# Where the causal mask is added in a fused two-layer attention kernel, and scores cut at the diagonal

## The chip, the cores and the metric

The kernel runs on one core of a Trainium2 chip. The metric is the device time in microseconds of one execution; a time given for a kernel is the median of its runs. A profile is one execution taken by the hardware profiler; it lists every instruction of the engines TensorE (PE; its weight loads are listed apart as PEld), VectorE (DVE), ScalarE (ACT), GpSimd (POOL) and SyncE (SP) with start and end.

## The reference, cut to what matters

There are two layers over x of shape 8 x 512 x 256. Each is x + attention(norm(x)) + ffn(norm(x)). Attention has 16 heads of 16 features over 512 tokens; the change touches that of layer 1, which is causal and is done twice on the same keys and values, the second time with queries that come out of a convolution over the first result:

```python
def _causal_attn(q, k, v):
    scale = 1.0 / math.sqrt(q.shape[-1])
    scores = jnp.einsum('bthd,bshd->bhts', q, k) * scale
    t = q.shape[1]
    mask = jnp.tril(jnp.ones((t, t), dtype=bool))
    scores = jnp.where(mask, scores, -jnp.inf)
    attn = jax.nn.softmax(scores, axis=-1)
    return jnp.einsum('bhts,bshd->bthd', attn, v)
...
ctx = _causal_attn(q, k, v)
conv_out = conv(ctx, conv_w, taps=3) + conv_b
ctx2 = _causal_attn(conv_out, k, v)
out = ctx2 @ out_w.T + out_b
```

Layer 0 has attention without a mask and a feed-forward part with eight routed experts; layer 1 a low-rank feed-forward part with gelu. Everything is in fp32.

## The kernel before, in words

Attention is cut into jobs (`Job`, L372) of one batch and four heads. Each head has 16 features, kept on 32 partitions, so that the four heads of a job lie on the four groups of 32 rows of TensorE, and the scores of up to four heads can run beside each other. Layer 0 has 32 jobs of 8 steps, layer 1 has 64 jobs of 6 steps (32 for the first attention, 32 for the second). All steps of both layers form one joined run of numbered steps (`run`, L490).

A job passes twice over its scores. In the first pass, `scores` (L384), queries lie on the partitions of the result; VectorE takes each row's maximum (L414, in layer 1 with a causal mask added from SBUF, L416). `shift` (L423) then transposes the maxima on TensorE (L426), VectorE copies them (L429), and four small DMAs on SP's queue (L433) write them into a spare row of the queries. In the second pass, `exps` (L435), twelve steps (`LEAD`) after the first, keys lie on the partitions, the shift is part of the product, and ScalarE takes the exponential out of the bank (L469). `attend` (L475) multiplies the exponentials with the values (L482).

In layer 1 a step of either pass works on two heads (one pair of row groups, `pr`), and the two passes of a step are on opposite pairs, so that four row groups are busy at once. What blocks a step takes is in `MX_SEQ` and `SC_SEQ` (L81 to L89): a block of keys `kc` needs only the queries from `lo = 128 kc` on, so key block 0 is 512 columns wide, block 1 is 384 and shares a bank with block 3 of 128, and block 2 is 256. The steps of a job take block 0, then blocks 3 and 1, then block 2, first for one pair of heads and then for the other. The first pass has the same widths in the same order.

The causal mask of the second pass concerns only the first 128 columns of each block, which lie on the diagonal. `mask_t` (L206) is two copies of a 128 x 128 triangle of 0 and -1e30 in bf16. In `exps`, after the scores of both heads, two matmuls (L463) with the bf16 identity as weights add `mask_t` to the bank: 128 columns per head for a step with one block, 256 for one with two. The exponentials wait for them. In a bank with two blocks, the one at column 128 is multiplied first, so that the mask's columns of both blocks are at the front.

The order of the work is the program's own (no scheduler moves instructions on an engine). A step is: scores of the first and the second pass, block by block in turn (L525, `zip` over both lists); then what follows each (maxima on VectorE; masks and exponentials); then filling work out of `todo` (L536); then the attends that are due. `fill_evenly` (L151) spreads the filling work (projections L347, values L356, convolution L1124, gelu part L1047 and L1075, transposes L320, L426 and L1142, output projection L1174) by due time and cost over the steps that are `free` (L508): four of each six. The other two have attends (key block 0 in one; 1, 3 and 2 in the next). So nearly every step has either filling work or attends behind its masks.

The PSUM banks are dealt out by rings (`share_banks`): in the joined run three banks for the first pass, three for the second (`sc`), one for the attends, one or two for the rest (L261, L265). At `t == end`, when the first passes are over, `banks_last` (L269) gives the second pass five.

In the twelve steps in which layer 1 has begun and the second pass still belongs to layer 0, the first pass has steps of two blocks and the second only of one. `zip` stops at the shorter list, so there the second block of the first pass, query chunk 0 of the first two jobs, isn't multiplied: 8 matmuls. The maxima of those rows are then those of what the bank held, which only changes by what the softmax is shifted.

Of the kernel before, what the change touches and what calls it, by code (L numbers as in the profile page):

```python
# [1 line left out]

# [17 lines left out]
P = 128  # L20
NB = 8
S = 512
# [5 lines left out]
PH = 32  # L28
# [52 lines left out]
SC_SEQ = (  # L81
    [((i // 2,), 1 - i % 2) for i in range(8)],
    [((0,), 0), ((3, 1), 0), ((2,), 0), ((0,), 1), ((3, 1), 1), ((2,), 1)],
    [((0,), 0), ((0,), 1), ((3, 1), 0), ((3, 1), 1), ((2,), 0), ((2,), 1)],
)
# [94 lines left out]
def block_kernel(ctx: ExitStack, tc: tile.TileContext, x, a0_wqk, a0_bqk, a0_wv, a0_bv, cent, experts,  # L180
                 a1_wqk, a1_bqk, a1_wv, a1_bv, conv_w, conv_b, out_w, out_b, u1, v1, f_b1, u2, v2, f_b2, out):
    nc = tc.nc
# [20 lines left out]
    ident_bf = const.tile([P, P], BF16, name="ident_bf")  # L203
    nc.vector.tensor_copy(ident_bf, ident)

    mask_t = const.tile([P, 2 * P], BF16, name="mask_t")  # L206
# [26 lines left out]
    def take_turn(kind):  # L233
        turn[kind].append(turn[kind].pop(0))
        return turn[kind][-1]
# [13 lines left out]
    def share_banks(**kinds):  # L249

        rings.update({k: list(v) for k, v in kinds.items()})

    def bank(kind="mm"):
        rings[kind].append(rings[kind].pop(0))
        return rings[kind][-1]
# [5 lines left out]
    def banks_alone():  # L261
        share_banks(mx=banks[:3], sc=banks[3:6], av=banks[6:7], mm=banks[7:])


    def banks_between(free):  # L265
        share_banks(mm=banks[6:] if free else banks[7:])


    def banks_last():  # L269
        share_banks(sc=banks[:5], av=banks[6:7], mm=banks[5:6] + banks[7:])  # L270
# [4 lines left out]
    class Norms:  # L275
# [4 lines left out]
        def __init__(self, pool, bs, nm, twice):  # L280
            self.bs, self.nm, self.twice = bs, nm, twice
            n = len(bs) * NC
            self.mv = pool.tile([P, n, 2], F32, name=f"mv{nm}", bufs=1)
            self.rs = pool.tile([P, 2 if twice else 1, n], F32, name=f"rs{nm}", bufs=1)
            self.rs1 = pool.tile([P, n], F32, name=f"rs1{nm}", bufs=1) if twice else None
            self.nm2 = pool.tile([P, n], F32, name=f"nn{nm}", bufs=1) if twice else None
            self.nm_t = pool.tile([P, n], F32, name=f"nm{nm}", bufs=1)
# [84 lines left out]
    class Job:  # L372


        def __init__(self, nm, causal, scale, v, g, done):
            self.nm, self.causal, self.scale, self.v, self.g, self.done = nm, causal, scale, v, g, done
            self.q = self.k = None
            self.m = None
            self.seq = int(causal)
            self.shift_row = (HD, 0)[g % 2]  # L380
            self.e = {}
            self.av = None

        def scores(self, i):  # L384
# [38 lines left out]
        def shift(self):  # L423
# [8 lines left out]
            for c in range(NC):  # L432
                nc.sync.dma_start(out=self.q[self.shift_row : P : PH, c * P : (c + 1) * P], in_=mT[4 * c : 4 * c + 4, :])  # L433

        def exps(self, i):  # L435
            blocks, pr = SC_SEQ[self.seq][i]
            heads = [bank("sc") for _ in range(2)]
            parts, at = [], 0
            for kc in blocks:
                lo = kc * P if self.causal else 0  # L440
                parts.append((kc, at, lo))
                at += S - lo
            mm = [
                [
                    lambda h=h, kc=kc, at=at, lo=lo: nc.tensor.matmul(  # L445
                        heads[h % 2][:, at : at + S - lo],
                        lhsT=self.k[h * PH : (h + 1) * PH, kc * P : (kc + 1) * P],
                        rhs=self.q[h * PH : (h + 1) * PH, lo:],
                        start=kc == blocks[-1],
                        stop=not self.causal,  # L450
                    )
                    for h in (2 * pr, 2 * pr + 1)
                ]
                for kc, at, lo in reversed(parts)
            ]
            n = at

            def after():
                if self.causal:


                    for h in range(2):
                        nc.tensor.matmul(  # L463
                            heads[h][:, : len(blocks) * P], lhsT=ident_bf, rhs=mask_t[:, : len(blocks) * P],
                            start=False, stop=True,
                        )
                e = take_turn("e" if n == S else "e2")
                for h in range(2):
                    nc.scalar.activation(e[:, h, :], heads[h][:, :n], AF.Exp, scale=self.scale)  # L469
                for kc, at, lo in parts:  # L470
                    self.e[kc, pr] = e[:, :, at : at + S - lo]

            return mm, after
# [16 lines left out]
    def run(jobs0, jobs1, todo):  # L490
        end = T0 + STEPS[1] * len(jobs1)
        for job in jobs1[-(LEAD // STEPS[1]) :]:
            job.seq = 2
        mx_at, sc_at, attends = {}, {}, {}
        for layer, jobs in enumerate((jobs0, jobs1)):
            for j, job in enumerate(jobs):
                t0 = layer * T0 + STEPS[layer] * j
                for i in range(STEPS[layer]):

                    t = t0 + i  # L500
                    mx_at.setdefault(t if t >= LEAD else t - t % 2, []).append((job, i))
                    t += LEAD
                    sc_at.setdefault(t if t < end else t - (t - end) % 2, []).append((job, i))
                av_at = AV_AT[job.seq]
                for i, blocks in av_at.items():
                    attends.setdefault(LEAD + t0 + i, []).append((job, blocks, i == max(av_at)))

        def free(t):  # L508

            return t < TS or 0 < (t - TS) % STEPS[1] < 5  # L510

        todo.first()
        for t in range(max(attends) + 1):
            todo.t = t
            if t == LEAD:
                banks_alone()
            if t == end:
                banks_last()
            mm, after = [], []
            for at, call in ((mx_at, Job.scores), (sc_at, Job.exps)):  # L520
                for job, i in at.get(t, ()):
                    m, a = call(job, i)
                    mm.append(m)
                    after.append(a)
            for together in zip(*mm):  # L525
                for m in together:
                    for f in m:
                        f()
            for f in after:
                f()  # L530
            if t >= end:
                todo.fill(t, 99.0, 1)
            elif "pool" in l1:
                if t >= TS + STEPS[1]:
                    banks_between(free(t))
                todo.fill_evenly(t, free)  # L536
            else:
                todo.fill(t, MOE_PER_STEP, 99)
            for job, blocks, last in attends.get(t, ()):
                for kc in blocks:  # L540
                    job.attend(kc, kc == 0, last and kc == blocks[-1])
                if last:
                    job.done(job, t)
        todo.drain()

    norms_of = {}
# [55 lines left out]
    if True:  # L602
# [338 lines left out]
        for b in range(NB):  # L941
            for g in range(HG):
                job = Job(f"0_{b}_{g}", False, 1.0, vbuf[b % 2], g, l0_done)
# [287 lines left out]
    for n in range(NB * HG + LAG):  # L1231
        if n < NB * HG:
            l1_job(1, n)
        if n >= LAG:
            l1_job(2, n - LAG)
    l1["ready"] = features_ready
    run(jobs, jobs1, todo)


# [86 lines left out]
```

## Time and profile before

| what | value |
|---|---|
| median of 3 runs | 2138.09 us (2135.71 to 2151.41) |
| the profiled execution: its own time | 2149.31 us |
| its span, first to last instruction | 2147.5 us |
| TensorE busy | 1984.3 us, 92% |
| VectorE, ScalarE, GpSimd busy | 1252.2, 995.2, 403.1 us |
| granted TensorE clock, mean | 0.974 |
| masks of the second pass (L463) | 768 matmuls |

How to read a profile's row of a group: line, engine, operation, out<-in by the program's names, rows x columns of the array and the shape, count; then busy time in us and the mean length of one in ns; then the engine's idle time just before such instructions and who ended it. Matmuls are pipelined and their ends are modelled, so the lengths of neighbours overlap: two starts are compared rather than a start and an end. An fp32 matmul of the program stands in the trace as two matmuls (two passes), a bf16 one as one. In a row of the timeline, equal neighbours are merged (x4), and the columns are start in us from the span's start, length in us, and what. A row of waits says who waited for whom: us in total, times, and the longest.

Slices of the span (a digit is the busy share in tenths of one of 40 slices of 53.7 us) show that layer 1, from about 1000 us on, has TensorE busy at 9 tenths and VectorE at 6.

### The profile page before, as it was taken

Reading aid. Unit: us, or ns where it says so; the run is one execution under the profiler, and the core shown is the slowest. Engines: PE = TensorE matmul, PEld = TensorE weight load, DVE = VectorE, ACT = ScalarE, POOL = GpSimd, SP = SyncE. Lnnn points to the kernel's source line nnn. Section 1 sums busy time; section 2 is a strip of 40 time slices with the busy share of each in tenths; the row PEclk is TensorE's granted clock in tenths of the full one; section 3 lists DMA queues with packets and bytes.
Section 4 is the critical chain, followed back from the end, with each engine's and each line's share of the span. In section 5 each row is a group of like instructions: output and inputs, shape, how many; then the busy total and the mean of one; then the engine's idle time right before and its main releaser. Section 6 shows DMA issues by size and latency. Waiting matters only on the chain. (4 is left out here: it accounts for less than half of the span.)

```text
span 2147.5 us, 36982 instructions
## 1 busy us (share of the span) xinstructions
PE 1984.3 (92%) x14168; PEld 1027.1 (48%) x14168; DVE 1252.2 (58%) x3611; ACT 995.2 (46%) x1950; POOL 403.1 (19%) x414
## 2 busy tenths in 40 slices
PE   5797999999999999988999999899999999999998
PEld 3333555555555555543444544445445444454554
DVE  5564455555545554555666666666666665666663
ACT  4343333333333333335456564555565555545554
POOL 4153000000000000024355321222121222212100
PEclk8699999999999999997999999999999999999999
DMA  5013212132222122121000000000000000000000
GB/s 209 13 47 119 104 52 104 62 122 77 67 99 94 63 94 104 57 53 40 16 16 15 8 2 2 12 2 2 11 2 11 2 2 11 2 2 12 2 12 21
DMA packets 37201, 93.64 MB, mean 44 GB/s; under 512 B 5920, under 2 KB 28064, under 8 KB 34080
## 3 DMA queue, kind: packets, MB, share of 16 engines
q0 software_dynamic: 6384, 59.78, 7.6%
q1 hardware_dynamic: 29792, 30.56, 4.5%
q8 instruction: 111, 1.82, 0.4%
q10 hardware_dynamic: 848, 0.93, 0.1%
q14 instruction: 66, 0.54, 0.1%
HBM read 70.03 MB, written 20.45 MB: 42 GB/s over the span
## 5 line engine op out<-in xcount | busy, mean ns | idle before, releaser
L469 ACT ACTIVATE e<-bank 128x512 f32<-128x512 f32 (+1 forms) x1280 | 639.4, 552 | 830.6 <-PE bank L445 480.5
L397 PE MATMUL bank<-k,q 32*128 32x512 f32 (+1 forms) x3056 | 724.5, 536 | 25.5 <-DVE m L414 23.6
L416 DVE CUSTOM_DVE_ANT_0 junk<-bank,cmask 128x512 bf16<-128x512 f32 (+3 forms) x1024 | 502.5, 491 | 352.3 <-PE bank L397 277.2
L445 PE MATMUL bank<-q,k 32*128 32x512 f32 (+3 forms) x3072 | 685.9, 531 | 3.4 <-ACT e L469 3.1
L397 PEld LDWEIGHTS bank<-k,q 32*128 32x128 f32 x3056 | 267.7, 186 | 410.2 <-issue 160.1
L414 DVE TENSOR_REDUCE m<-bank 128x1 f32<-128x512 f32 x512 | 328.9, 685 | 159.2 <-PE bank L445 127.8
L482 PE MATMUL bank<-e,v 128*32 128x512 f32 (+3 forms) x3072 | 305.9, 500 | 8.9 <-ACT k L339 2.9
L445 PEld LDWEIGHTS bank<-q,k 32*128 32x128 f32 x3072 | 250.0, 185 | 16.5 <-ACT e L469 9.6
L1065 POOL TENSOR_SCALAR xT<-xT 128x512 f32<-128x512 f32 x64 | 95.3, 1489 | 605.5 <-ACT xT L1057 524.7
L829 PE MATMUL bank<-hsT,w 128*128 128x256 f32 x736 | 182.4, 394 | 6.9 <-DVE hsT L812 6.9
L829 PEld LDWEIGHTS bank<-hsT,w 128*128 128x128 f32 x736 | 135.5, 192 | 74.9 <-issue 59.1
L850 PE MATMUL bank<-w,hT 128*128 128x256 f32 x736 | 169.1, 383 | 0.0
L850 PEld LDWEIGHTS bank<-w,hT 128*128 128x128 f32 x736 | 136.1, 190 | 36.4 <-issue 19.7
L347 PE MATMUL bank<-xT,wqk 128*128 128x256 f32 (+1 forms) x384 | 134.2, 479 | 11.9 <-DVE q L337 4.8
L938 POOL TENSOR_TENSOR acc<-acc,og 128x256 f32<-128x256 f32 x32 | 23.2, 725 | 591.2 <-DVE og L934 591.1
L482 PEld LDWEIGHTS bank<-e,v 128*32 128x32 f32 x3072 | 71.5, 109 | 113.8 <-issue 89.4
L463 PE MATMUL bank<-mask_t,ident_bf 128*128 128x128 bf16 (+1 forms) x768 | 122.9, 243 | 0.0
L463 PEld LDWEIGHTS <-ident_bf 128*128 128x128 bf16 x768 | 43.9, 97 | 155.0 <-issue 139.7
L1124 PE MATMUL bank<-ctxT,cw 128*128 128x128 f32 x768 | 100.4, 281 | 13.1 <-DVE mT L429 11.2
L842 DVE TENSOR_SCALAR hT<-bank,w 128x256 f32<-128x256 f32 x92 | 44.5, 484 | 115.5 <-ACT hT L840 115.5
L1124 PEld LDWEIGHTS bank<-ctxT,cw 128*128 128x128 f32 x768 | 92.0, 194 | 23.3 <-DVE mT L429 14.3
L347 PEld LDWEIGHTS bank<-xT,wqk 128*128 128x128 f32 x384 | 68.8, 196 | 70.1 <-issue 42.2
(178 smaller groups left out, 1702.6 us busy)
## 6 DMA issues: line engine op xcount, KB each, us to landing
q<-mT SPq DMA_DIRECT2D x384, 2.0 KB
hs_d<-zeros SPq DMA_DIRECT2D x23, 256.0 KB
hs<-hs_d SPq DMA_DIRECT2D x23, 256.0 KB
fs_d<-f SPq DMA_DIRECT2D x23, 256.0 KB
acc<-in_x SPq DMA_DIRECT2D x8, 512.0 KB
out<-acc SPq DMA_DIRECT2D x8, 512.0 KB
cw<-in_conv_w SPq DMA_DIRECT2D x1, 768.0 KB
wqk<-in_a_wqk ACTq DMA_DIRECT2D x1, 512.0 KB
```

The source lines that it names most:

```text
L347: nc.tensor.matmul(ps, lhsT=w[:, k, col : col + P], rhs=src[:, k, tokens], start=(k == 0), stop=(k == 1))
L397: lambda h=h, qc=qc, at=at, nk=nk: nc.tensor.matmul(heads[h % 2][:, at : at + nk], lhsT=self.q[h * PH : (h + 1) * PH, qc * P : (qc + 1) * ...
L414: nc.vector.tensor_reduce(self.m[:, qc, h, :], src, AX.X, ALU.max, negate=True)
L416: nc.vector.tensor_tensor_reduce(out=l1["junk"][:, :nk], in0=src, in1=l1["cmask"][:, S - nk :], scale=1.0, scalar=-3e38, op0=ALU.add, op1= ...
L445: lambda h=h, kc=kc, at=at, lo=lo: nc.tensor.matmul(heads[h % 2][:, at : at + S - lo], lhsT=self.k[h * PH : (h + 1) * PH, kc * P : (kc + 1 ...
L463: nc.tensor.matmul(heads[h][:, : len(blocks) * P], lhsT=ident_bf, rhs=mask_t[:, : len(blocks) * P], start=False, stop=True,)
L469: nc.scalar.activation(e[:, h, :], heads[h][:, :n], AF.Exp, scale=self.scale)
L482: nc.tensor.matmul(self.av[h * PH : (h + 1) * PH, lo:], lhsT=self.v[:, kc, 4 * self.g + h, :], rhs=es[h // 2][:, h % 2, :], start=first, s ...
L829: nc.tensor.matmul(ps[:, i * TB : (i + 1) * TB], lhsT=w[:, O_W1 + k * FF + fc * P : O_W1 + k * FF + (fc + 1) * P], rhs=self.hsT[:, k, :], ...
L850: nc.tensor.matmul(ps[:, 0:D], lhsT=self.hT[:, fc, j * P : (j + 1) * P], rhs=w[:, O_W2 + fc * D : O_W2 + (fc + 1) * D], start=(fc == 0), s ...
L1065: nc.gpsimd.tensor_scalar(c, c, 1.0, None, ALU.add)
L1124: nc.tensor.matmul(ps, lhsT=l1["cw"][:, k, tap, c * P : (c + 1) * P], rhs=l1["ctxT"][b % 2][:, k, tap + lo : tap + lo + P], start=(k == 0 ...
```

## The change

The masks leave the end of `exps` for a function of their own, `masks`. It takes the two banks, and writes the mask into the first columns of both as the first matmuls of their group (`start=True`). `run` calls it at the end of a step, after filling work and attends, for the second pass of the next step. The scores then add to what the mask wrote. For this each block is cut at the diagonal: 128 columns that lie on the mask, and the rest, which are fresh columns. So a step's scores of 512 columns become pieces of 384 and 128; those of blocks 1 and 3 become 256, 128 and 128; those of block 2 become 128 and 128. The last piece to be issued is the diagonal one of the first block.

`zip` becomes `zip_longest`, since the lists of both passes now differ in length in every step; the eight left-out matmuls of the first pass are so put in. `banks_last` is called at the end of the step before `end`, ahead of the masks for `end`.

```diff
+        def masks(self, i):
+            n = len(SC_SEQ[self.seq][i][0]) * P
+            self.banks[i] = heads = [bank("sc") for _ in range(2)]
+            for h in heads:
+                nc.tensor.matmul(h[:, :n], lhsT=ident_bf, rhs=mask_t[:, :n], start=True, stop=False)
+
         def exps(self, i):
             blocks, pr = SC_SEQ[self.seq][i]
-            heads = [bank("sc") for _ in range(2)]
+            heads = self.banks.pop(i) if self.causal else [bank("sc") for _ in range(2)]
...
+            n = at
+            pieces = [(kc, at, lo, S) for kc, at, lo in parts]
+            if self.causal:
+                pieces = [(kc, at, lo, lo + P) for kc, at, lo in parts]
+                pieces += [(kc, at + P, lo + P, S) for kc, at, lo in parts if lo + P < S]
             mm = [
                 [
-                    lambda h=h, kc=kc, at=at, lo=lo: nc.tensor.matmul(
-                        heads[h % 2][:, at : at + S - lo],
+                    lambda h=h, kc=kc, at=at, lo=lo, hi=hi: nc.tensor.matmul(
+                        heads[h % 2][:, at : at + hi - lo],
                         lhsT=self.k[h * PH : (h + 1) * PH, kc * P : (kc + 1) * P],
-                        rhs=self.q[h * PH : (h + 1) * PH, lo:],
-                        start=kc == blocks[-1],
-                        stop=not self.causal,
+                        rhs=self.q[h * PH : (h + 1) * PH, lo:hi],
+                        start=not self.causal,
+                        stop=at == 0,
                     )
                     for h in (2 * pr, 2 * pr + 1)
                 ]
-                for kc, at, lo in reversed(parts)
+                for kc, at, lo, hi in reversed(pieces)
             ]
-            n = at
             def after():
-                if self.causal:
-                    for h in range(2):
-                        nc.tensor.matmul(
-                            heads[h][:, : len(blocks) * P], lhsT=ident_bf, rhs=mask_t[:, : len(blocks) * P],
-                            start=False, stop=True,
-                        )
                 e = take_turn("e" if n == S else "e2")
...
-            if t == end:
-                banks_last()
...
-            for together in zip(*mm):
+            for together in zip_longest(*mm, fillvalue=()):
...
                 if last:
                     job.done(job, t)
+            if t + 1 == end:
+                banks_last()
+            for job, i in sc_at.get(t + 1, ()):
+                if job.causal:
+                    job.masks(i)
```

More of the change, by code (lines that the diff above doesn't have):

```diff
@@ L1 @@
 from contextlib import ExitStack
+from itertools import zip_longest
 import concourse.bass as bass
@@ L381, in __init__ @@
             self.e = {}
+            self.banks = {}
             self.av = None
```

## The prediction

> **What bounds the kernel now.** I read the page's busy shares first, then the busy time by stretch, then the waits of layer 1, then TensorE's instructions in order of time.
>
> ```profile
> PE 1984.3 (92%) x14168; PEld 1027.1 (48%) x14168; DVE 1252.2 (58%) x3611; ACT 995.2 (46%) x1950; POOL 403.1 (19%) x414
> L463 PE MATMUL bank<-mask_t,ident_bf 128*128 128x128 bf16 (+1 forms) x768 | 122.9, 243 | 0.0
> ```
>
> ```profile
> 1500.00:1600.00 100.00, 94.43 (x834) 49.41 (x834) 66.04 (x236) 56.17 (x116) 18.86 (x13) 1.00 0.02 7
> ```
>
> Columns of the second: TensorE, its weight loads, VectorE, ScalarE, GpSimd, then granted clock and DMA. Layer 1 runs from about 1000 us to the end; its 384 steps of 2.75 us keep TensorE 94% busy at the full clock, so what an edit does to the order of TensorE's own work counts almost fully, unless TensorE waits there anyway. Its waits in layer 1:
>
> ```profile
> PE bank L1124 <- DVE mT L429: 11.2, 12, 1.7
> PE bank L426 <- ACT avs L1158: 7.0, 12, 1.9
> PE bank L445 <- ACT e L469: 2.6, 6, 1.2
> ACT e L469 <- PE bank L463: 335.4, 270, 4.5
> ```
>
> TensorE mostly waits for VectorE to empty the bank of the transposed maxima (L429). For the exponentials it hardly waits, although ScalarE waits 335 us for the mask: ScalarE has the slack. Then the steps themselves (start, length, what):
>
> ```profile
> 1506.63 0.28 PE L463 MATMUL bank<-mask_t,ident_bf 128*128 128x128 bf16 x2
> 1506.85 1.50 PE L482 MATMUL bank<-e,v 128*32 128x384 f32 x24
> 1508.28 0.59 PE L397 MATMUL bank<-k,q 32*128 32x384 f32 x2
> ...
> 1509.36 0.39 PE L463 MATMUL bank<-mask_t,ident_bf 128*128 128x256 bf16 x2
> ...
> 1515.03 0.70 PE L397 MATMUL bank<-k,q 32*128 32x512 f32 x2
> ...
> 1516.11 0.28 PE L463 MATMUL bank<-mask_t,ident_bf 128*128 128x128 bf16 x2
> ```
>
> The lengths overlap, so I use start to next start. Two things are to be seen. A group of scores of one 512-wide block per head takes 1516.11 - 1515.03 = 1.08 us, and one made of a 384 and a 128 block takes 1509.36 - 1508.28 = 1.08 us too. And the price of a mask depends on what stands behind it, as these show:
>
> ```profile
> 1018.31 1.13 PE L347 MATMUL bank<-xT,wqk 128*128 128x256 f32 x4
> 1019.37 0.59 PE L397 MATMUL bank<-k,q 32*128 32x384 f32 x2
> ...
> 1244.91 0.39 PE L463 MATMUL bank<-mask_t,ident_bf 128*128 128x256 bf16 x2
> 1245.14 1.03 PE L347 MATMUL bank<-xT,wqk 128*128 128x256 f32 x4
> 1246.10 0.48 PE L397 MATMUL bank<-k,q 32*128 32x256 f32 x2
> ...
> 1322.86 0.28 PE L463 MATMUL bank<-mask_t,ident_bf 128*128 128x128 bf16 x2
> 1322.98 1.04 PE L320 MATMUL bank<-ident,o 128*128 128x128 f32 x8
> ```
>
> The same projection, four passes of 256 columns, takes 1.06 us straight behind scores (1018.31) and 0.96 behind a mask (1245.14). The 0.10 is the load of its first weights, which lies bare after a change of tile shape, and which the mask covers today. So a narrow mask in front of a fill of full tile shape costs only 0.12 (1322.86 to 1322.98), of which 0.10 would be paid anyhow. In front of the attends (other tile shape, so TensorE empties first) it costs 0.22 (1506.63 to 1506.85).
>
> **The change part by part.** No other engine's instruction list changes; TensorE gets 776 more fp32 matmuls (768 pieces, 8 maxima), and its masks move.
>
> *Masks moved.* The prices: a 256-wide pair followed at once by scores took 0.322, a narrow pair followed by scores 0.215, in both about 0.10 of it the emptying of the array; so the columns alone are about 0.215 and 0.11. Counting the neighbours of each mask pair in TensorE's instruction order, before:
> - 123 narrow in front of attends x 0.215 = 26.4
> - 115 wide in front of fills x 0.229 = 26.3
> - 61 narrow in front of full-shape fills x 0.122 = 7.4
> - 61 narrow in front of gelu fills of another shape (L1047, L1075) x 0.215 = 13.1
> - 12 with no fill = 3.5; together 76.7 us.
>
> After (the mask stands behind the fill or the attends, in front of scores):
> - 157 narrow behind full-shape fills x 0.11 = 17.3; 38 wide x 0.215 = 8.2
> - 61 narrow behind attends x 0.215 = 13.1; 62 wide x 0.322 = 20.0
> - 23 wide behind L1047 x 0.322 = 7.4; 18 narrow behind narrow shapes x 0.215 = 3.9; 13 with no fill 2.9
> - and the bare first weights of 116 full-shape fills that now follow scores, x 0.10 = 11.6; the 63 transposes of maxima (L426) load 16 columns instead of 128, taken as 0.02 each = 1.3 (bounds 0 and 6.3).
>
> Together 85.7, so +9.0 us. The mask itself is not dearer; what it hid comes bare. The bounds are 0 (the load of the first weights goes partly behind the emptying) and +19 (0.05 more in each of 384 steps, should mask and scores not overlap as fill and scores do).
>
> *Cover lost in waiting steps.* In 64 steps the fill then waits for VectorE (45.9 us in all). Going through them, 11.9 us of the mask's time lay inside what would otherwise have been a longer wait. VectorE's queue is set by the scores, whose end does not move, so the fill waits that much longer and the mask comes on top behind it: +11.9, less 3 for bare weights that vanish in the same waits: +9 (bounds 0, if the next step's VectorE queue gives it back, and +12).
>
> *Split scores.* A piece more on the two row groups of the exponentials, while the maxima's row groups run their 512 or 384 + 128 columns. The trace has that very pair of pieces, at 1.08 against 1.08; to the nanosecond the medians are 7 to 9 ns apart: 384 x 0.008 = +3 us. A rule speaks against it: the Trainium skill, TensorEngine Tiling (Array Packing), section Performance Considerations (Instruction Overhead), gives each matmul some 60 cycles on trn2, 25 ns at the 2.4 GHz it states. With 388 pairs of pieces, two passes each, side by side in pairs, that would be an estimated +19 us, and the sum +37. I take the row, which is of this shape, and keep the rule for the range. What the trace lacks is two row groups going through three pieces while the two others do two.
>
> *Masks ahead of the bank.* The ring of scores has three banks in this stretch. The second mask of a step therefore waits for the first exponential of the step before. Behind it in TensorE's queue stand the maxima's scores, and behind these VectorE; before, only the exponentials' own scores waited, and the maxima ran meanwhile. In 53 of 368 steps the first exponential ends after the next scores begin. There a wait now costs mask and emptying behind it, about 0.2; but the exponentials begin earlier, since they no longer wait for the mask: they start 0.27 (narrow) or 0.32 us (wide) after the scores' group today, and 0.17 after it in layer 0, which has no mask (the median of 211 groups); so 0.10 to 0.15 earlier. In about half of the 53 ScalarE is behind with older work and nothing is gained; but the scores of all four row groups then run together, where a late pair ran on alone. Going through the 63 steps that come within reach of it, wins and losses leave +1; bounds -6 (0.1 in 60) and +12 (0.2 in 60). If ScalarE's slack were gone, each late exponential would delay the next step one for one.
>
> *Missing maxima.* Eight 128-wide matmuls in four steps, beside 512-wide scores of layer 0 on the other row groups: 1.07 us either way: 0.
>
> *The end.* In the last 35 us the chain of waits goes scores, mask, exponential, copy; the exponential comes 0.15 to 0.3 earlier some four times: -1.
>
> Sum: 9 + 9 + 3 + 1 - 1 = +21 us on the profiled execution's span of 2147.5 us (2149.3 with what lies around it), or 0.98%. The median of the runs, 2138.1, stands 0.5% below that execution, so I scale: 2138.1 x 1.0098 = 2159 us.
>
> **The rivals.**
> *The shorter chain wins (not slower).* Exponentials that start 0.12 earlier take away waits. For it: 24 us by which score groups are stretched where ScalarE is late, and 25 us of ScalarE waits in fills. Against it: in 315 of 368 steps the exponential is done in time. At 0.12 in each of 100 such places it is -12, which leaves 2147. If all 49 us went, because a wait breaks a longer queue behind it, 2138 + 21 - 49 = 2110; it is faster than before once more than 21 us of the 49 go.
> *Splitting is dear.* If the loads of the extra pieces are not hidden, each costs 0.107 (the bare load above): 388 pairs x 2 passes x 0.107 = +83, 2239 at the worst; by the rule, 2175. For it: the loads in a 128-wide chain have just 0.107 us of columns to hide behind. Against it: 128-wide passes follow each other today at 0.11 (1509.03 and 1509.14 in order of time).
> *Nothing to see.* The lost cover is given back by shorter VectorE waits later: +3 to +8, 2141 to 2146: masks that lie in front of the scores give the waiting engines the time that the fills lose.
>
> **How the numbers follow.** My sum 0.60, the chain 0.15, dear pieces 0.17, nothing 0.08. A change within 1% is about what a measurement of this kernel cannot tell from none; the edge is 2159.5. The sum has 2159 in its middle, and its terms' bounds added at their worst are -25 and +24, of which I expect half: so 0.30 over the edge and 0.30 within. The chain gives 0.10 faster and 0.05 within, dear pieces 0.17 slower, nothing 0.08 within: faster 0.10, same 0.43, slower 0.47. Range: 2122 leaves out the strong half of the chain, 2190 the worse part of dear pieces; the sum's own range is 2147 to 2171.
>
> **What would show it.** Right: score groups still 1.08 and 0.65; projections straight behind scores 1.06; narrow masks 0.11 longer than the fill without one; ScalarE starting 0.17 after the scores; more wait at L429's readers. Wrong: score groups of 1.15 or more (pieces are dear), or ScalarE's late steps gone and the fills' waits smaller (the chain).

## The result, and the profile after

The changed kernel took 2169.07 us (median of 4 runs, 2162.67 to 2172.55) beside 2141.91 of the kernel before: ratio 1.012, interval 1.007 to 1.0169. Run again it gave 2172.56 beside 2149.17, ratio 1.0112 (1.0088 to 1.0137). So it is 1.1% slower, about +24 us; forecast was +21 and 2159. The profiled execution has a span of 2170.3 us, 22.8 more.

These are two lines of the page after, the engines' shares and the masks (the last columns of the second line are its wait and for whom), then the same stretch as in the prediction:

```profile
PE 1970.7 (91%) x15720; PEld 1130.0 (52%) x15720; DVE 1248.7 (58%) x3611; ACT 993.0 (46%) x1950; POOL 403.0 (19%) x414
L443 PE MATMUL bank<-mask_t,ident_bf 128*128 128x128 bf16 (+1 forms) x768 | 129.0, 240 | 21.8 <-ACT e L476 19.8
```

```profile
1500.00:1600.00 100.00, 91.96 (x946) 58.97 (x942) 64.65 (x231) 55.76 (x116) 18.85 (x13) 1.00 0.02 7
```

TensorE has 1552 rows more and yet is busy 14 us less over the span, and it waits more: it is busy in 92% of this stretch, 94% before. The other engines do what they did. The waits of layer 1 after:

```profile
PE bank L443 <- ACT e L476: 19.8, 27, 1.7
PE bank L1134 <- DVE mT L431: 14.4, 13, 1.9
PE bank L428 <- ACT avs L1168: 8.6, 12, 2.1
```

The wait of the masks for the exponential of the step before is new; that for the copy of the maxima (L429, now L431) has grown from 11.2 at its largest reader to 14.4, and over all its readers from 31.3 to 43.1. Where that comes from is seen in one job's second step. In the kernel before, behind the mask at 1509.36 that the prediction shows, and in the changed one:

```profile
1511.64 0.66 PE L1142 MATMUL bank<-ident,avs 128*128 128x128 f32 x4 [0.91 <-DVE mT L429]
```

```profile
1515.06 1.50 PE L489 MATMUL bank<-e,v 128*32 128x384 f32 x24
1516.49 0.39 PE L443 MATMUL bank<-mask_t,ident_bf 128*128 128x256 bf16 x2
1516.82 0.59 PE L399 MATMUL bank<-k,q 32*128 32x384 f32 x2
...
1517.90 0.28 PE L428 MATMUL bank<-ident,m 128*16 128x128 f32 x1
...
1520.17 0.66 PE L1152 MATMUL bank<-ident,avs 128*128 128x128 f32 x4 [1.12 <-DVE mT L431]
```

From the end of the scores to the transposes L1142 (L1152) it is 1511.64 - 1509.36 = 2.28 us before and 1520.17 - 1517.90 = 2.27 after. The wait for VectorE's copy sets that time, and the mask of 0.23 lay inside it. Now the mask stands between attends and scores, where it costs 1516.82 - 1516.49 = 0.33 and nothing hides it. The wait in brackets has grown by 0.21, which is the mask that is gone.

The bare weights, and the mask behind a fill:

```profile
1529.24 1.13 PE L1184 MATMUL bank<-ow,xT 128*128 128x256 f32 x4
1530.21 1.03 PE L348 MATMUL bank<-xT,wqk 128*128 128x256 f32 x4
1531.07 0.28 PE L443 MATMUL bank<-mask_t,ident_bf 128*128 128x128 bf16 x2
1531.28 0.48 PE L399 MATMUL bank<-k,q 32*128 32x256 f32 x2
```

These are two fills of the same size: the one straight behind scores takes 0.97 us, the second 0.86. The narrow mask takes 0.21 to the scores, of which 0.10 is the emptying of the array that would have stood between fill and scores anyway.

### The profile page after: what moved, and what is told of

It reads as the page before. It is cut to its first block, busy times and chain, and to the rows that moved or that the text cites. A ratio compares the mean times of both kernels' runs of the same rounds, so it can differ in the third digit from the quotient of the medians.

```text
span 2170.3 us, 40019 instructions
## 1 busy us (share of the span) xinstructions
PE 1970.7 (91%) x15720; PEld 1130.0 (52%) x15720; DVE 1248.7 (58%) x3611; ACT 993.0 (46%) x1950; POOL 403.0 (19%) x414
## 5 line engine op out<-in xcount | busy, mean ns | idle before, releaser
L399 PE MATMUL bank<-k,q 32*128 32x512 f32 (+3 forms) x3072 | 709.9, 535 | 25.9 <-DVE m L416 25.1
L461 PE MATMUL bank<-q,k 32*128 32x128 f32 (+3 forms) x4608 | 677.3, 409 | 0.4 <-ACT e L476 0.4
L399 PEld LDWEIGHTS bank<-k,q 32*128 32x128 f32 x3072 | 261.2, 186 | 303.0 <-issue 102.9
L461 PEld LDWEIGHTS bank<-q,k 32*128 32x128 f32 x4608 | 348.8, 186 | 41.1 <-issue 3.4
L443 PE MATMUL bank<-mask_t,ident_bf 128*128 128x128 bf16 (+1 forms) x768 | 129.0, 240 | 21.8 <-ACT e L476 19.8
L443 PEld LDWEIGHTS <-ident_bf 128*128 128x128 bf16 x768 | 61.3, 98 | 126.5 <-issue 112.0
L1134 PE MATMUL bank<-ctxT,cw 128*128 128x128 f32 x768 | 101.1, 282 | 16.6 <-DVE mT L431 14.4
L348 PEld LDWEIGHTS bank<-xT,wqk 128*128 128x128 f32 x384 | 67.9, 193 | 70.9 <-issue 40.3
```

The lines of the kernel that those rows point to most:

```text
L348: nc.tensor.matmul(ps, lhsT=w[:, k, col : col + P], rhs=src[:, k, tokens], start=(k == 0), stop=(k == 1))
L399: lambda h=h, qc=qc, at=at, nk=nk: nc.tensor.matmul(heads[h % 2][:, at : at + nk], lhsT=self.q[h * PH : (h + 1) * PH, qc * P : (qc + 1) * ...
L443: nc.tensor.matmul(h[:, :n], lhsT=ident_bf, rhs=mask_t[:, :n], start=True, stop=False)
L461: lambda h=h, kc=kc, at=at, lo=lo, hi=hi: nc.tensor.matmul(heads[h % 2][:, at : at + hi - lo], lhsT=self.k[h * PH : (h + 1) * PH, kc * P : ...
L1134: nc.tensor.matmul(ps, lhsT=l1["cw"][:, k, tap, c * P : (c + 1) * P], rhs=l1["ctxT"][b % 2][:, k, tap + lo : tap + lo + P], start=(k == 0 ...
```

## The experiments

Each run is compared with the kernel before in its own set of runs (2139.72, 2149.17 or 2141.52 us); between sets only ratios and differences are compared. Where I give a number "without the throttle", each run's time is lessened by its span x (1 - its granted clock), which is at most what a clock below full speed took, and the means are compared; this sets runs side by side that drew different clocks. For the changed kernel run again it gives +24.0 us.

**The changed kernel again.** 

> The changed kernel once more, for a narrower interval: its four runs gave a ratio of 1.012 (1.007 to 1.0169). By the per-step times of its profile with the clock's share taken out it should be +16 to +20 us, ratio 1.008 to 1.010; if the throttle has no part in it, 1.012.

Measured: as above, 1.0112, and clocks alike (0.9752 and 0.9750). So 24 us is the size here, and the throttle has no part in it; the lower guess was wrong.

**Only the cutting, with the maxima.**

```diff
-                        start=not self.causal,
-                        stop=at == 0,
+                        start=(kc, at) == pieces[-1][:2] or not self.causal,
+                        stop=not self.causal,
...
             def after():
+                if self.causal:
+                    for h in range(2):
+                        nc.tensor.matmul(
+                            heads[h][:, : len(blocks) * P], lhsT=ident_bf, rhs=mask_t[:, : len(blocks) * P],
+                            start=False, stop=True,
+                        )
...
-            for job, i in sc_at.get(t + 1, ()):
-                if job.causal:
-                    job.masks(i)
```

> Only the scores are cut at the diagonal; the masks stay behind them as before, and the maxima are put in. My theory (what moves costs, the pieces do not): groups of scores 0.01 us longer, 1.09 and 0.66 us, so +4 us, ratio 1.002. Rival, pieces are dear (25 ns for each matmul): +19 us, ratio 1.009, and groups of 1.13 us. Second rival, the whole +27 us of the change is the cutting: ratio 1.012.

Measured: 2140.06 beside 2139.72, ratio 0.9998 (0.998 to 1.0016); without the throttle +3.2. In the trace the score groups' medians went up by 0.008 to 0.013 us, 371 of them, +3.8. Both rivals fall (the 25 ns are the 60 cycles that the prediction weighed; the trace's own figure is near, 256 mask columns in 0.107 us): neither the pieces nor the maxima are the loss.

**Ahead in the last step alone.**

```diff
-                if job.causal:
+                if job.causal and job.seq == 1 and i == 5:
                     job.masks(i)
```

In the other five steps the scores stay whole and the mask stays behind them.

> The mask goes ahead in the last step of each job alone (i = 5), where it moves from in front of attends (0.215 us today) to behind a full-shape fill (0.11 us). My theory: 62 x 0.105 = -6.7 us, ratio 0.997, faster than before. Rival, a mask ahead costs the same wherever it is (+27 us over six steps): +4.5 us, ratio 1.002.

Measured: 2139.19 beside 2139.72, ratio 1.0003 (0.9987 to 1.002); without the throttle -1.0. A miss: the 6.7 us did not come. A line of its waits:

```profile
PE bank L443 <- ACT e L483: 10.2, 13, 1.5
```

The mask waits for the exponential of the fifth step. That wait was there before, as stretched scores of the sixth: scores whose second pair runs on late because its bank is not yet free. They took 13.0 us before and none now, so the exchange alone costs nothing. By the trace the fifth step (i = 4) grew by 20.4 us, where 6.6 for the mask's columns and 11.0 of waits make 17.6; the sixth shrank by 22.8, where 13.0 and the mask's 13.3 make 26.3. So some 6 us are missing in these two steps, which is the gain that did not come. What took them is not shown.

**Ahead in the second step alone**, the same edit with `i == 1`. 

> The mask goes ahead in the second step of each job alone (i = 1, two blocks), where it moves from in front of the transpose of the maxima, whose readers wait for VectorE anyway, to behind the attends of the step before. My theory: 62 x 0.322 added = 20.0, 62 x 0.229 = 14.2 taken away, but about 10 of these 14 lay in waits, so +16 us, ratio 1.0075. If no cover is lost: +6 us, ratio 1.003. Rival, a mask ahead costs the same everywhere: +4.5 us. Rival, the earlier exponential is worth something: below +6.

Measured: 2156.02 beside 2139.72, ratio 1.0073 (1.0045 to 1.0101), +16, as forecast; without the throttle it is +20.6. One mask in six makes two thirds of the loss or more. Its largest wait for the copy of the maxima, 11.2 us in 12 waits before:

```profile
PE bank L1141 <- DVE mT L431: 14.7, 13, 1.9
```

Over all readers these waits grew from 31.3 to 40.3 us, most of the way to the 43.1 of the changed kernel.

**Ahead in all steps but the second.** 

> The changed kernel, but the mask of the second step (i = 1) stays behind its scores, in front of the transpose of the maxima. My theory now, that nearly all of the loss comes from that one step, where the mask had cost nothing: no slower than before, ratio 0.998 to 1.002. Rival, the loss is spread over the steps by bare weights and emptying: five sixths of it stay, +15 to +20 us, ratio 1.007 to 1.010.

Measured: 2156.03 beside 2149.17, ratio 1.0028 (1.0012 to 1.0044); without the throttle +6.3. Against 1.0112 three quarters of the loss are gone. The waits for the copy of the maxima are back near the old value, 33.4 us. "No slower" was too good, though: some 6 us are spread over the other steps.

**No masks at all, in the kernel before.** 

> The kernel before with the masks of the second pass left out (and the scale of those exponentials made 20 times smaller, so that they stay finite): it measures what the masks cost where they stood. My theory: 76.7 us of masks, less 12 for first weights that come bare in 114 full-shape fills, less 12 that lay in waits for VectorE: about -53 us, ratio 0.975. Rival, the masks also held up the exponentials and these held up TensorE: all 77 us and up to 49 us of waits, ratio 0.964 or less.

Measured: 2118.28 beside 2139.72, ratio 0.9886 (0.9859 to 0.9913): -24, and without the throttle -32. Both theories missed. The masks take 77 us of TensorE's time by their rows, but leaving them out gains under half of it. TensorE's waits in layer 1 rose from 77.2 to 117.4 us. Two of its lines:

```profile
PE bank L426 <- ACT avs L1150: 19.1, 27, 2.3
PE bank L474 <- ACT q L339: 4.9, 13, 0.5
```

The first was 7.0 us in 12 waits with the masks, the second (L482 then) 1.9 in 7. So some 40 us of masks lay in time that TensorE would have waited, not the 12 I had counted. I had counted masks beside waits for VectorE that the trace shows. A mask that just fills a wait leaves none to be seen: in fills and attends TensorE waits 165 times without the masks, 120 times with them. And most of the growth is in waits for ScalarE (26.0 to 48.7 us), which I had not counted at all.

Sums over 62 jobs of the time from each step's scores to the next step's, without the throttle, in us. In the last row this time holds the mask of the next step in place of the step's own: that of step 0 holds the wide mask of the second step.

| step i | 0 | 1 | 2 | 3 | 4 | 5 |
|---|---|---|---|---|---|---|
| before | 171.4 | 200.7 | 187.2 | 178.4 | 178.8 | 139.9 |
| no masks, less before | -11.8 | -1.3 | -1.1 | -8.4 | -10.0 | 0.0 |
| after (again), less before | +6.8 | +9.3 | -1.7 | +8.6 | +8.3 | -8.7 |

With all masks gone, steps 1, 2 and 5 took nearly as long as before: there TensorE's waits in fills and attends grew by 12, 9 and 8 us, and its stretched scores by 3, 1 and 5. The last row is from the second profile of the changed kernel. The first gives +7.9, +5.3, -3.0, +6.9, +8.3 and -9.2, so an entry is good to some 4 us.

**The second step's mask left out, before and after.** 

> The kernel before with the masks of the second step of each job (i = 1) left out (and the scale of layer 1's exponentials made 20 times smaller, so that they stay finite): what this mask costs where it stood. Its columns are 62 x 0.229 = 14.2 us. If TensorE's waits in this step hide it where there are any (29 steps, 6.6 us) and partly where it only just has none: -2 to -7 us, ratio 0.997 to 0.999. Rival, nothing hides it: -14 us, ratio 0.9935.

> The changed kernel with the same masks left out (and the same small scale): what they cost in their new place, behind the attends of the step before. My theory: 62 x 0.322 = 20 us and some 2 to 5 of waits for the exponential of the step before, which nothing hides: -20 to -25 us against the changed kernel, so ratio 1.000 to 1.002 to the kernel before. Rival, in the new place VectorE's waits give it back later: -10 us or less, ratio 1.006 or more.

Measured: in the kernel before 2139.44 beside 2141.52, ratio 0.9984 (0.9967 to 1.0), -3.4 us of the mask's 14.2, without the throttle -0.7: most of it was hidden. What stood behind this mask, the transpose of the maxima, now waits for ScalarE instead (7.0 us in 12 waits before):

```profile
PE bank L426 <- ACT avs L1157: 14.0, 19, 2.2
```

In the changed kernel 2151.13, ratio 1.0045 (1.0029 to 1.0062); against 1.0112 that is -14, between the two expectations. Its clock was lower (0.9729, that of the kernel before 0.9763); without the throttle it is +2.3 beside +24.0, so -22, as my theory has it. The same mask costs 1 to 3 us in the one place and 14 to 22 in the other.

**The copy of the maxima on ScalarE**, before and after.

```diff
-                nc.vector.tensor_scalar(mT, ps[0 : 4 * NC, 0:P], -1.0, None, ALU.mult)
+                nc.scalar.activation(mT, ps[0 : 4 * NC, 0:P], AF.Identity, scale=-1.0)
```

> The kernel before, with the copy of the transposed maxima of layer 1 (L429) done by ScalarE. It starts 1.72 us after the transpose today, behind four maxima on VectorE; behind two exponentials of 0.54 us on ScalarE it should start at about 1.25. My theory, that these waits set the second step: up to 0.47 x 45 steps = -21 us, less what the later exponentials cost, so -10 to -20 us, ratio 0.991 to 0.995. Rival, the waits only move to the next bank or to ScalarE's late steps: 0.

> The changed kernel with the same copy on ScalarE. If the mask's move costs because the wait for VectorE in the second step had hidden the mask, then with a shorter wait less is hidden: +8 to +14 us over the same edit of the kernel before, instead of +17 to +27. If the loss has nothing to do with that wait: the same difference as between the two kernels without the edit.

Measured: on the kernel before 2123.19 beside 2149.17, ratio 0.9894 (0.9871 to 0.9917), -23 us, without the throttle -18: a version that beats both kernels. On the changed one 2146.56, ratio 0.9999 (0.9987 to 1.0011). The difference between the two is 0.0105 x 2149 = 23 us, without the throttle 20, beside 24 for the change without the edit. So my expectation for the second, 8 to 14, fell. A wait of the edited kernel before, the same in the edited changed one, and the stretch of the first:

```profile
PE bank L1124 <- ACT mT L429: 5.0, 10, 0.7
PE bank L1134 <- ACT mT L431: 5.4, 10, 0.8
```

```profile
1500.00:1600.00 100.00, 96.30 (x866) 50.96 (x865) 67.46 (x236) 61.56 (x129) 24.37 (x17) 1.00 0.02 7
```

In the second step TensorE waits in 29 jobs with the edit as without, 0.68 us each instead of 1.13: there the waits became shorter, not fewer. Moving the masks now lengthens the waits for the copy by 1.6 us (11.5 to 13.1 over all readers) where it was 12 without the edit. So little cover was left in this one wait, as the test meant, and yet the loss fell by 1 to 4 us only. Other waits in fills and attends took its place: those for the rest of VectorE's and ScalarE's work grew by 11.6 us, where it was 7 to 9 without the edit. The test therefore speaks against the copy of the maxima as the one wait that matters. Why the others grew is not shown.

## Why the prediction was right, step by step

*Masks moved, +9.* Confirmed in its prices, the sum itself was not measured apart: medians of 0.215 and 0.322 behind attends, 0.205 and 0.312 behind full-shape fills with about 0.10 of emptying in each, and 116 fills whose first weights lie bare for 0.1045, at most 12.1 us (worked out: 11.6; 27 of them come after a wait).

*Cover lost, +9.* Right in kind, too small by half and outside its bounds of 0 and +12. TensorE's waits in fills and attends went from 73.4 us to 90.9 and, in the second profile, 94.7: +17 to +21. The step that failed is the count of the mask's time inside waits, 11.9 us. It took in the waits for VectorE alone, and the waits for the copy of the maxima did grow by about as much, 11.8 and 12.5. But those for VectorE's other work grew too, by 1.9 and 5.5 us, and those for ScalarE, put at nothing, by 4.9 and 3.7. Nor did the 3 us come off that bare weights were to save. In the second step the fills waited in 29 jobs before and in 28 and 29 after, only longer (1.10 us each, then 1.37 and 1.34): the waits there did not grow in number.

*Split, +3.* Confirmed: +3.2 without the throttle, +3.8 by the groups. The rule of the Trainium skill that was weighed (TensorEngine Tiling (Array Packing), Performance Considerations (Instruction Overhead)) does not hold here if it is read as 60 cycles on top of each piece: that would have been +19, outside the run's interval. A piece beside longer work on other row groups cost 0.008 to 0.013 us for each group of scores. Steps with three pieces beside two, which the trace before lacked, are among the groups that took 0.010 more.

*Masks ahead of the bank, +1.* Wrong in sign and outside its bounds of -6 and +12. By the kind of step, exponentials start 0.19 to 0.25 us after the scores (medians; 0.27 to 0.38 before, 0.17 expected), so 0.04 to 0.13 earlier, where 0.10 to 0.15 was expected. The stretched score groups vanish, 32.4 to 2.2 us, for 21.3 us of new waits at the masks: -9. In the second profile it is -7. The prediction counted 24 us of stretched groups and let wins and losses cancel.

These two terms, too small by 10 and too large by 9, miss in opposite directions, so that the sum stands so near to the measurement is in part luck. With what was measured for the terms it is 9 + 19 + 3.5 - 8 = 23.5 beside 24.0 of the runs. In the profiles themselves layer 1's steps grew by 16 and 23 us, where the same sum gives 21 and 27, so the terms are not known to better than 4 or 5 us.

*Maxima, 0.* With the cutting they gave a ratio of 0.9998.

*The end, -1.* Not measured by itself.

*The rivals.* The shorter chain did take away waits for ScalarE, but two thirds of them came back at the masks. Dear pieces fell with the run of the cutting alone. Something was given back only in steps 2 and 5 (-1.7 and -8.7), and not by shorter waits for VectorE, as the rival had it: there the stretched scores went (10.0 and 13.0 us before, under 1 after).

What stays open: how the spread +6 us of the other steps divides between bare weights and waits; why the loss stayed near 20 us with the copy on ScalarE, when the wait for the copy no longer grew; why the last step's mask, moved alone, gained nothing; and why the second step's mask in its new place came to -14 by the runs and -22 without the throttle.

## What to carry to other kernels

Work that stands where its engine would wait anyway costs little or nothing, and a trace shows only what is left of such a wait: here 12 us of cover beside waits that could be seen, some 40 in all. Before moving such work, ask what the engine would wait for if it were gone, on every other engine, and leave it out once to measure that. A small instruction in front of another of the same tile shape can also hide the other's first weight load. Moved to the far side, it lays that load bare (0.1045 us here) and becomes no cheaper itself (0.12 before, 0.11 and the emptying after). And a removed wait can come back one instruction later: of some 30 us of stretched scores, 21 to 24 came back as waits at the masks.

## What the runs showed of the hardware

The part ahead of layer 1's first exponential differs by eight small matmuls and the place of the first masks, yet took 1045.3 us in the profiled execution before and 1050.8 in that after, 1051.9 in the second one, and 1036.1 with the copy on ScalarE. The granted clock of that part was 0.959, 0.953, 0.953 and 0.972. The records show stretches of half clock of 3.4 us or multiples of it, and how many fell there changed from execution to execution: span x (1 - clock) of this part was 42.7 us before and 49.5 after. So the 5.5 us by which it grew between the first two profiles, out of 22.8, can be of this kind, and not the change's. A change of tile shape cost about 0.10 us of emptying (0.205 of a narrow mask, less the 0.107 of its columns, which is what 128 columns more for each head add: 0.312) and, in front of fp32 work with 128 weight columns, 0.1045 of bare weight load (49 places with 256 columns to stream: 0.320 us from the first matmul to the second, 0.216 between fills).
